# Layer 1 from its second quarter on: scores and sums in four square corners of the TensorE array, even destination blocks before odd ones

## The chip, the core and the metric

The kernel runs on one core of a Trainium2 chip. TensorE (PE) multiplies matrices into the eight banks of PSUM; VectorE (DVE) and ScalarE (ACT) do element work; GpSimd (POOL) and SyncE (SP) issue DMAs here. The metric is the device time of one execution in microseconds (us). The three runs of the kernel before gave 795.45, 795.53 and 796.22, so the median is 795.53.

## The reference, cut to what matters

Four graph layers work on 4096 nodes with 64 features each; every layer normalises its input and adds its result. Layer 0 sums neighbours with decaying weights, layer 1 is an attention, layer 2 is two gated steps, layer 3 is a midpoint in hyperbolic space. The change is in layer 1:

```python
h = lorentz_linear(x, W, b, scale)
q = lorentz_linear(h, Wq, bq, scale_q)
k = lorentz_linear(h, Wk, bk, scale_k)
qm = jnp.concatenate([-q[:, :1], q[:, 1:]], axis=-1)
att = 2.0 + 2.0 * (qm @ k.T)
att = jax.nn.sigmoid(att / att_scale + att_bias)
att = adj * att
support = att @ h
...
return support / denorm
```

`adj` is a dense 4096 x 4096 matrix. The fast path of the kernel needs every entry to be 0 or 1, because it keeps the matrix as 8-bit floats; it checks this on the chip, and falls back on a general path if a check fails.

## The kernel before

**Tiling.** The nodes are 32 blocks of 128 (`NB`), and four quarters of 1024 destinations (`NQ` is 4). A quarter's destinations are dealt out alternately to two halves of 512 columns (`c` = 0 even blocks, `c` = 1 odd blocks; `CW` is 512). `A8[q][i]` holds the adjacency of quarter `q` for the source blocks 2i and 2i+1.

**Layer 1** (`stream1`, from line 1360). For each quarter `q`, pair of source blocks `i` (0 to 15) and half `c`:
- `score` (line 1332) multiplies the keys of two source blocks with the queries of 512 destinations. The contraction is 64 long, so the two blocks use the upper and the lower half of the array's rows (64 rows x 128 columns each) at the same time, into two PSUM banks.
- `weigh` (line 1341) takes two sigmoids on ScalarE out of PSUM and multiplies them by the adjacency on VectorE, into the tile `sig`.
- `add` (line 1364) sums: the source block's 64 features are the columns, so the two blocks use the left and the right half of the array's columns (128 rows x 64 columns each), and add into the two partition halves of the PSUM bank `acc[c]`.

All of these matmuls are in fp32; one such matmul is two records in the trace. The loop takes two pairs `i` at a time: four calls of `score` (both halves, two pairs), then four of `add` for pairs that came earlier, so that the array changes its shape twice a round. `evac` (line 1062) adds the two partition halves of both banks when a quarter is done, and `post1` (line 1417) computes the rest of that quarter, with one transpose before (`ps_n`) and one after (`ps_t`).

**What sets the order.** Everything runs in the order that the program is written in, engine by engine; `Weave` (line 606) writes it. It keeps a planned clock for each engine from fixed costs per operation (`cost`, `book_pe`), and holds side work as generators that yield one operation at a time. `draw` and `fill` insert side work where the plan says that it begins early enough; `finish` issues all that is left of the main side work. `weave.back` is side work of the lowest rank, and is left out while `weave.quiet` is set.

**The checks** (`checks`, line 1113) are that lowest-ranked work. Each of 128 checks loads a 128 x 1024 piece of the adjacency (512 KB, tile `whole`) and has VectorE test that it holds only zeros and ones. The tiles `whole` and `sig` share one pool of six buffers (`b4p`). When layer 3 begins its last part, `layer3` (line 1736) issues every check that is left at once, before its sums go on; after them a small matmul (`flag_ps`) and a copy give the flag that the end of the program reads.

**The end.** Layer 3 computes eight units of 512 destinations. `take3` moves a unit's sums out of PSUM, on ScalarE and then VectorE (`n<-n,acc`; a tile `n65`). `head3` and `post3` (line 1848) then run a long chain of small operations, three units together, then three, then one (unit 6), then the last (`last3`). The Newton steps of a reciprocal root (`guess`, `nt`, `nu`, `ny`) and a polynomial for artanh (`po`, `at`) are in it, and each is one small VectorE instruction after the other.

In the trace, L984 is every matmul (`mm`), L988 every transpose (`turn4`), and L785 every operation that the planner records, so groups are told apart by their tiles.

Of the kernel before, what the change touches and what calls it, by code (L numbers as in the profile page):

```python
# [12 lines left out]
AF = mybir.ActivationFunctionType  # L13
ALU = mybir.AluOpType
# [4 lines left out]
P = 128  # L19
D = 64  # L20
NH = 2
CW = 512
# [13 lines left out]
def general_kernel(ctx: ExitStack, tc: tile.TileContext, t: dict, out: bass.AP):  # L36
# [48 lines left out]

    X = []
    x_nm = t["x"]
    for h in range(NH):
        xh = keep.tile([P, HB, D], F32, name=f"X{h}")
        nc.sync.dma_start(xh, x_nm[:, h * HB:(h + 1) * HB, :])  # L90
        X.append(xh)

# [42 lines left out]
    def nm_tile(name="nm", **kw):  # L135
        return nm.tile([P, HB, D], F32, tag=kw.pop("tag", "nm"), name=name, **kw)

    def stat(name="st"):
        return small.tile([P, HB], F32, tag="st", name=name)
# [5 lines left out]
    def sumsq(v, w=D):  # L145
        sq = nm_tile("sq")
        nc.vector.tensor_tensor(sq[:, :, :w], v, v, ALU.mult)
        s = stat("ss")
        nc.vector.tensor_reduce(s, sq[:, :, :w], AX.X, ALU.add)
        return s  # L150
# [11 lines left out]
    def relu_ln(xh, dst):  # L162

        m = stat("mean")
        nc.vector.tensor_reduce(m, xh, AX.X, ALU.add)
        nc.vector.tensor_scalar(m, m, 1.0 / D, None, op0=ALU.mult)
        xc = nm_tile("xc")
        nc.vector.tensor_tensor(xc, xh, rows(m), ALU.subtract)
        v = sumsq(xc)
        nc.vector.tensor_scalar(v, v, 1.0 / D, LN_EPS, op0=ALU.mult, op1=ALU.add)  # L170
        nc.scalar.activation(v, v, AF.Sqrt)
        nc.vector.scalar_tensor_tensor(dst, xc, 0.0, rows(recip(v)), op0=ALU.max, op1=ALU.mult)
# [20 lines left out]
    def fm_tile(name="fm", **kw):  # L193
        return feat.tile([D + 1, HN], F32, tag=kw.pop("tag", "fm"), name=name, **kw)
# [89 lines left out]
    def pre0(h):  # L284
        hn = nm_tile("h0")
        relu_ln(X[h], hn)
        fm = fm_tile("h0T")
# [282 lines left out]
NQ = 4  # L570
QB = 8
# [30 lines left out]
def names(*aps):  # L602
    return [a.tensor.name for a in aps if isinstance(a, bass.AP)]


class Weave:
# [53 lines left out]
    def free(self, ps):  # L660
        k = ps.tensor.name
        self.banks[self.kind.pop(k)].append(self.used[k][0])
# [7 lines left out]
    def add(self, gen, back=False):  # L670
        piece = [gen, None]
        (self.back if back else self.work).append(piece)
        self.step(piece, None)
# [123 lines left out]
def fast_kernel(ctx: ExitStack, tc: tile.TileContext, t: dict, out: bass.AP, flag: bass.AP):  # L797
# [13 lines left out]
    NB = N // P  # L811
# [10 lines left out]
    weave = Weave()  # L822
    free = weave.free

    def one(name):
        return weave.take(1, lambda: psp.tile([P, CW], F32, tag="one", name=name, bufs=8))

    def several(names_):
        return [one(n) for n in names_]

    def b2(name, shape=(P, QB, D), dtype=F32):
        return b2p.tile(list(shape), dtype, tag="b2", name=name)
# [6 lines left out]
    DV, AC, GP, SY = (Engine(weave, x.e, x.real, True) for x in (V, S_, G_, Y_))  # L839
# [132 lines left out]
    def book_pe(o, lhsT, rhs, passes):  # L972
        k, m, n = lhsT.shape[0], math.prod(lhsT.shape[1:]), math.prod(rhs.shape[1:])
        tiled = (k < P) + 2 * (m < P)
        dur = max(0.42e-3 * n * passes * (0.5 if tiled else 1.0) * (0.5 if k < P and m < P else 1.0), 0.09)
        if passes > 1 and not tiled:
            dur += 0.05 if passes == 2 else 0.075
        weave.book("P", dur + ((0.18 if passes == 4 else 0.115) if tiled != weave.tiled else 0.0), names(lhsT, rhs), names(o))
        weave.tiled = tiled

    def mm(o, lhsT, rhs, start=True, stop=True):
        weave.wait(names(lhsT, rhs), names(o))
        book_pe(o, lhsT, rhs, 4 if lhsT.dtype == F32 else 1)
        nc.tensor.matmul(o, lhsT, rhs, start=start, stop=stop, skip_group_check=True)  # L984
# [31 lines left out]
    def flat(v):  # L1016
        return v.rearrange("p b d -> p (b d)")
# [19 lines left out]
    DONE = set()  # L1037
# [24 lines left out]
    def evac(acc):  # L1062

        lo, hi = slice(0, D), slice(D, P)
        a, mt = b2("agg", (P, CW)), b2("mt", (P, CW))
        sides = ((lo, hi), (hi, lo))
        for ps, (own, other) in zip(acc, sides):
            yield AC.activation(mt[own, :], ps[other, :], AF.Copy)
        for ps, (own, other) in zip(acc, sides):
            yield DV.tensor_tensor(a[own, :], ps[own, :], mt[own, :], ALU.add)  # L1070
            free(ps)
        return a
# [182 lines left out]
    S1, kT = {}, {}  # L1255
# [67 lines left out]
    qd = {}  # L1323

    def load1(q):
        if q < NQ:
            qd[q] = [b2("qd", (P, CW)) for _ in range(2)]
            for c in range(2):
                for half in (slice(0, D), slice(D, P)):
                    Y_.dma_start(qd[q][c][half, :], q_spill[q][c * D:(c + 1) * D, :])  # L1330

    def score(q, i, c):
# [5 lines left out]
            mm(ps[j], kb[half, :], qd[q][c][half, :])  # L1338
        return ps

    def weigh(q, i, c, ps):

        g = b4p.tile([P, 2, CW], F32, tag="b4", name="sig")
        for j in range(2):
            S_.activation(g[:, j, :], ps[j], AF.Sigmoid, bias=att_add, scale=att_mul)
            free(ps[j])
        v = g.rearrange("p k (j n) -> p k j n", n=P)
        a = A8[q][i].rearrange("p k (j c n) -> p k c j n", c=2, n=P)[:, :, c]
        V.tensor_tensor(v, v, a, ALU.mult)
        return g  # L1350
# [9 lines left out]
    def stream1():  # L1360

        acc, behind = [], []

        def add(c, q, i, gs):
            if i == 0:
                acc.append(one(f"acc{c}"))
            for j in range(2):
                b = 2 * i + j
                mm(acc[c][j * D:(j + 1) * D, :], S1[b // QB][:, b % QB, :], gs[c][:, j, :],
                   start=i == 0, stop=i == NB // 2 - 1)  # L1370

        def add_behind(more=()):
            q, i, gs = behind.pop(0)
            for c in (0, 1):
                add(c, q, i, gs)
                if more:
                    more.pop(0)()
                weave.draw(weave.quiet)
            if i == NB // 2 - 1:
                weave.finish()  # L1380
                weave.add(post1(q, acc[:]))
                acc.clear()

        def turn(q, i, later=None):
            if q == 0 and i % (QB // 2) == 0:
                weave.until((1, i // (QB // 2)), DONE)
            weave.quiet = (1, NQ - 1) not in DONE
            weave.late = 2.0 if weave.quiet else 0.8
            gs = ahead[:] if (q, i) == (0, 0) else []
            for c in range(len(gs), 2):  # L1390
                ps = score(q, i, c)
                if later is None:
                    gs.append(weigh(q, i, c, ps))
                else:
                    later.append(lambda q=q, i=i, c=c, ps=ps: gs.append(weigh(q, i, c, ps)))
                weave.draw(weave.quiet or c == 1)
            behind.append((q, i, gs))
            if i == 8:
                load1(q + 1)

        for q in range(NQ):
            for i in range(0, NB // 2, 2):

                later = []
                turn(q, i)
                turn(q, i + 1, later)
                while len(behind) > 2:
                    add_behind(later)
                for go in later:
                    go()  # L1410
                if len(behind) > 1:
                    add_behind()
        add_behind()

    X = {}

    def post1(q, acc):
        a = yield from evac(acc)
        X[q] = b2(f"X{q}")
        yield SY.dma_start(flat(X[q]), x_spill[q])  # L1420
        sup = b2("sup")
        ps = yield from to_nm(a)
        sq = b2("sq")
        yield AC.activation(sq, ps, AF.Square)
        yield AC.activation(sup, ps, AF.Copy)
        free(ps)
        s = stat("space", QB)
        yield DV.tensor_reduce(s, sq[:, :, 1:], AX.X, ALU.add)
        yield DV.tensor_tensor(s, s, sq[:, :, 0], ALU.subtract)
        a = stat("abs", QB)  # L1430
        yield DV.tensor_scalar(a, s, -1.0, 1e-8, op0=ALU.mult, op1=ALU.max)
        yield DV.tensor_tensor(s, s, a, ALU.max)
        r = yield from rsqrt(s)
        yield DV.tensor_tensor(sup, sup, rows(r), ALU.mult)
        yield DV.tensor_tensor(X[q], X[q], sup, ALU.add)

        g = b2("g0")
        yield from relu_ln(X[q], g)
        yield from split3(g, 1.0, *parts(2, q), psum=False)
        DONE.add((2, q))  # L1440
        gT = b2("gT", (P, CW))
        yield from transpose4(g, gT)
        yield from spill2(q, 0, gT)
# [537 lines left out]
```

## Time and profile before

| what | value |
|---|---|
| median of the runs | 795.53 us |
| the profiled execution's own time | 796.44 us |
| its span, first to last instruction | 794.7 us |
| mean granted TensorE clock | 0.993 |
| first score of the second quarter | 305.05 us |
| last matmul record of layer 1's sums, end | 487.49 us |
| sums of layer 3 end, last stretch of TensorE | 779.7 us |
| checks on VectorE | 128, back to back 1.145 us apart |
| load of one check's piece, issue to landing | 6.7 us median |

The durations in the profile are of this one execution. "Busy" is the union of an engine's instructions; matmuls are pipelined, so that the distance between two starts, and not the duration of one, says what a matmul costs in a stream. A row of the timeline merges equal instructions that follow each other: start, length from the first start to the last end, engine, line, operation, what it writes and reads, shape, and count; in brackets, the idle time before it and what ended that. In a table of windows, an engine's number is its busy time, and in parentheses its count of instructions; the last three columns are clock, DMA share and GB/s.

### The profile page before, as it was taken

The numbers are of one execution on the slowest core, as the hardware profiler recorded it, in microseconds if no ns is written. First come the engines' busy times: TensorE is split into PE (matmuls) and PEld (weight loads), VectorE is DVE, ScalarE is ACT, GpSimd is POOL, SyncE is SP. The second block draws the span as 40 slices with busy tenths as digits, with TensorE's granted clock in tenths as the row PEclk, the third lists the DMA queues.
The fourth block names the chain that finished last, engine by engine and source line by source line (L and its number), as shares of the span: only waits on it lengthen the run. The fifth ranks groups of instructions, "written<-read, shape, count | busy, mean of one in ns | idle before, by whom it ended". The sixth has DMA issues, their size and how long they took to land.

```text
span 794.7 us, 12336 instructions
## 1 busy us (share of the span) xinstructions
PE 764.4 (96%) x4494; PEld 370.7 (47%) x4494; DVE 636.3 (80%) x1436; ACT 428.3 (54%) x759; POOL 62.1 (8%) x129
## 2 busy tenths in 40 slices
PE   6899999999999999999999999999999999999992
PEld 2344444444543433333333333444444444699992
DVE  5886867778779888898998997877779678786886
ACT  5565556555567677788787784122220235444333
POOL 4333232232000000000000000000000000000000
PEclk9999999999999999999999999999999999999997
DMA  9999999999710022113103007695788800000000
GB/s 192 162 188 178 222 164 194 220 163 209 203 45 31 10 69 77 41 31 104 53 27 106 27 27 254 202 340 174 254 307 305 287 14 14 2 2 1 15 28 18
DMA packets 44100, 98.54 MB, mean 124 GB/s; under 512 B 5120, under 2 KB 20608, under 8 KB 44032
## 3 DMA queue, kind: packets, MB, share of 16 engines
q1 hardware_dynamic: 25888, 78.98, 29.4%
q0 software_dynamic: 15984, 14.56, 19.6%
q10 hardware_dynamic: 2160, 4.14, 1.4%
q8 instruction: 37, 0.61, 0.3%
q14 instruction: 31, 0.25, 0.1%
HBM read 136.06 MB, written 5.24 MB: 178 GB/s over the span
## 4 chain that ended last, share of the span: by engine, by line
PE 84%; DVE 8%; ACT 3%; DMA 2%; issue 1%; SPq 0%; ACTq 0%; DVEq 0%
PE acc L984 52%; PE score L984 13%; PE cnt L984 12%; PE rz L984 2%; PE ps_l L984 1%; ACT sig L785 1%; PE ps_t L988 1%; DVE ss L785 1%; DVE sig L785 1%; PE ih L984 1%; DMA x<-in_x 1%; DVE nt L785 1%; ACT w L785 1%; PE ps_kq L984 1%; DVE w L785 1%
## 5 line engine op out<-in xcount | busy, mean ns | idle before, releaser
L785 ACT ACTIVATE sig<-score,fatt_add,fatt_mul 128x512 f32<-128x512 f32 x256 | 177.2, 784 | 47.8 <-PE score L984 40.8
L785 DVE TENSOR_TENSOR sig<-sig,A 128x1024 f32<-128x1024 f32 x128 | 155.0, 1224 | 23.5 <-ACT sig L785 17.7
L785 ACT ACTIVATE w<-cnt 128x512 int16<-128x512 f32 x198 | 111.4, 595 | 90.7 <-PE cnt L984 87.8
L785 DVE SCALAR_TENSOR_TENSOR whole<-whole 128x1024 f32<-128x1024 f32 x128 | 153.2, 1220 | 6.3 <-DMA whole<-in_adjT 5.9
L984 PE MATMUL score<-qd,kT 64*128 64x512 f32 x512 | 124.3, 609 | 0.0
L984 PE MATMUL acc<-sig,S 128*64 128x512 f32 x512 | 118.9, 600 | 1.4 <-DVE sig L785 1.2
L984 PEld LDWEIGHTS <-hm 128*128 128x128 bf16 x768 | 73.5, 98 | 92.1 <-issue 9.3
L984 PE MATMUL acc<-A,hm 128*128 128x512 fp8e4 x512 | 115.4, 379 | 0.0
L984 PE MATMUL cnt<-A,ftri 128*128 128x512 fp8e4 x256 | 97.8, 385 | 7.4 <-ACT A L785 5.8
L984 PE MATMUL cnt<-A,fupd 128*128 128x512 fp8e4 x248 | 95.2, 384 | 4.9 <-DVE w L785 1.9
L984 PE MATMUL acc<-S,A 128*128 128x196 bf16 x1024 | 88.4, 246 | 1.3 <-DVE S L785 1.3
L984 PEld LDWEIGHTS <-A 128*128 128x128 fp8e4 x1024 | 87.0, 97 | 2.2 <-DVE S L785 1.5
L984 PEld LDWEIGHTS score<-qd,kT 64*128 64x128 f32 x512 | 50.8, 186 | 68.2 <-issue 55.2
L984 PE MATMUL acc<-w,hm 128*128 128x512 bf16 x256 | 75.5, 379 | 0.3 <-DVE hm L785 0.3
L785 DVE TENSOR_SCALAR w<-cnt 128x512 int16<-128x512 f32 x58 | 40.1, 691 | 39.8 <-PE cnt L984 38.5
L868 POOL DMA_DIRECT2D A<-in_adjT x111 | 60.0, 543 | 129.3 <-DMA A<-in_adjT 128.1
L984 PEld LDWEIGHTS acc<-sig,S 128*64 128x64 f32 x512 | 33.1, 136 | 78.9 <-issue 58.2
L984 PEld LDWEIGHTS <-lo 128*64 128x64 bf16 x768 | 39.6, 109 | 49.6 <-issue 18.8
L984 PE MATMUL acc<-A,lo 128*64 128x512 fp8e4 x512 | 57.9, 380 | 0.0
L785 ACT ACTIVATE mt<-acc 64x512 f32<-64x512 f32 x32 | 18.9, 592 | 64.7 <-PE acc L984 64.1
L984 PEld LDWEIGHTS <-ftri 128*128 128x128 bf16 x256 | 24.8, 98 | 45.3 <-issue 21.2
L984 PEld LDWEIGHTS <-fupd 128*128 128x128 bf16 x248 | 24.4, 98 | 38.4 <-issue 14.0
(187 smaller groups left out, 611.5 us busy)
## 6 DMA issues: line engine op xcount, KB each, us to landing
whole<-in_adjT SPq DMA_DIRECT2D x128, 512.0 KB, 6.7
A<-in_adjT POOLq DMA_DIRECT2D x111, 128.0 KB, 13.7
qd<-qs SPq DMA_DIRECT2D x16, 128.0 KB, 4.9
mx<-gs SPq DMA_DIRECT2D x16, 128.0 KB, 8.0
xT<-gs SPq DMA_DIRECT2D x8, 256.0 KB, 7.4
x<-in_x SPq DMA_DIRECT2D x6, 256.0 KB, 6.7
xs<-x SPq DMA_DIRECT2D x4, 256.0 KB, 5.9
qs<-qT ACTq DMA_DIRECT2D x4, 256.0 KB, 4.5
```

The lines of the kernel that those rows point to most:

```text
L785: return fn(*args, **kw)
L868: nc.gpsimd.dma_start(A8[q][b // 2][:, b % 2, :], a)
L984: nc.tensor.matmul(o, lhsT, rhs, start=start, stop=stop, skip_group_check=True)
L988: nc.tensor.transpose(o, src, ident)
```

## The change

The first quarter stays as it is. From the second quarter on, a new function `rest` runs the stream:

- `score4` cuts a pair's score matmuls into four of 64 rows x 64 columns: row half `r` is the source block as before, column half `h` is half of its 128 nodes. The two banks come out as before.
- `sum4` cuts the sums into four of 64 x 64: row half `r` is half of a source block's nodes, column half `k % 2` is the block of the pair. Bank `r` receives the sums over its half of the nodes; the result of one half of destinations is now spread over both banks and both partition halves.
- All even destination blocks of a quarter (`c` = 0, all 16 pairs) run first, then all odd ones.
- One score group and one sum group alternate; the sums run three steps behind the scores.
- `evac4` runs twice a quarter and adds the four partial sums together: a ScalarE copy of a bank (128 x 512), a VectorE sum, a ScalarE copy across partition halves (64 x 512), a VectorE sum. `evac` ran once, with two ScalarE copies and two VectorE sums of 64 x 512.
- `weave.quiet` and `weave.late` are set once, before `rest`; `load1` for the next quarter is called at the start of the odd blocks.

```diff
+    corners = [(slice(r * D, (r + 1) * D), slice(h * D, (h + 1) * D)) for r in range(2) for h in range(2)]
+
+    def score4(q, i, c):
+
+        kb = kT[i // 4][:, (i % 4) * P:(i % 4 + 1) * P]
+        ps = several(("score", "score"))
+        for j, (r, h) in enumerate(corners):
+            mm(ps[j // 2][h, :], kb[r, h], qd[q][c][r, :])
+        return ps
+
+    def sum4(acc, i, g):
+
+        for k, (r, h) in enumerate(corners):
+            b = 2 * i + k % 2
+            mm(acc[k // 2][h, :], S1[b // QB][r, b % QB, :], g[r, k % 2, :],
+               start=i == 0, stop=i == NB // 2 - 1)
...
+        def rest():
...
+            def close(q, c, ps):
+                if c == 0:
+                    halves[q] = b2("agg", (P, CW))
+                    weave.add(evac4(halves[q], ps, c))
+                else:
+                    weave.finish()
+                    weave.add(post1(q, ps))
...
+            for q in range(1, NQ):
+                for c in (0, 1):
+                    for i in range(NB // 2):
+                        g = weigh(q, i, c, score4(q, i, c))
+                        weave.draw(False)
+                        sums.append(lambda q=q, c=c, i=i, g=g: sums_of(q, c, i, g))
+                        if len(sums) > 3:
+                            pop()
+                        if (c, i) == (1, 0):
+                            load1(q + 1)
+            while sums:
+                pop()
+
+        for q in range(1):
...
-        add_behind()
...
+        weave.until((1, NQ - 1), DONE)
+        weave.quiet, weave.late = False, 0.8
+        rest()
...
+    def evac4(a, acc, c):
+
+        own, other = [slice(0, D), slice(D, P)][::1 - 2 * c]
+        t = b2("mt", (P, CW))
+        yield AC.activation(t, acc[0], AF.Copy)
+        free(acc[0])
+        yield DV.tensor_tensor(t, acc[1], t, ALU.add)
+        free(acc[1])
+        yield AC.activation(a[own, :], t[other, :], AF.Copy)
+        yield DV.tensor_tensor(a[own, :], t[own, :], a[own, :], ALU.add)
+
     def post1(q, acc):
-        a = yield from evac(acc)
+        if q in halves:
+            a = halves[q]
+            yield from evac4(a, acc, 1)
+        else:
+            a = yield from evac(acc)
```

More of the change, by code (lines that the diff above doesn't have):

```diff
@@ L1378, in add_behind @@
                 weave.draw(weave.quiet)
[L1379 to L1382, printed above, removed]
         def turn(q, i, later=None):
@@ L1398, in turn, with last, sums_of, pop @@
             if i == 8:
-                load1(q + 1)
-        for q in range(NQ):
+                load1(1)
+        def rest():
+            q0, i0, gs = behind.pop(0)
+            def last():
+                add(1, q0, i0, gs)
+                weave.finish()
+                weave.add(post1(q0, acc[:]))
+                acc.clear()
+            sums = [lambda: add(0, q0, i0, gs), last]
+            def close(q, c, ps):
[3 more added lines that the diff above has]
+                else:
+                    weave.finish()
+                    weave.add(post1(q, ps))
+            def sums_of(q, c, i, g):
+                if i == 0:
+                    acc[:] = several(("acc0", "acc1"))
+                sum4(acc, i, g)
+                if i == NB // 2 - 1:
+                    close(q, c, acc[:])
+                    acc.clear()
+            def pop():
+                sums.pop(0)()
+                weave.draw()
+            for q in range(1, NQ):
[11 more added lines that the diff above has]
+        for q in range(1):
             for i in range(0, NB // 2, 2):
@@ L1412, in stream1 @@
                     add_behind()
-        add_behind()
-    X = {}
-    def post1(q, acc):
-        a = yield from evac(acc)
+        weave.until((1, NQ - 1), DONE)
+        weave.quiet, weave.late = False, 0.8
+        rest()
+    X, halves = {}, {}
+    def evac4(a, acc, c):
[7 more added lines that the diff above has]
+        yield DV.tensor_tensor(a[own, :], t[own, :], a[own, :], ALU.add)
+    def post1(q, acc):
+        if q in halves:
[3 more added lines that the diff above has]
+            a = yield from evac(acc)
         X[q] = b2(f"X{q}")
```

## The prediction

> **What bounds the kernel now.** I read the page first (busy time, chain), then layer 1 on TensorE in order of time, then the VectorE queue at the very end. The page and its chain of waits:
>
> ```profile
> PE 764.4 (96%) x4494; PEld 370.7 (47%) x4494; DVE 636.3 (80%) x1436; ACT 428.3 (54%) x759; POOL 62.1 (8%) x129
> ...
> PE 84%; DVE 8%; ACT 3%; DMA 2%; issue 1%; SPq 0%; ACTq 0%; DVEq 0%
> ...
> L984 PE MATMUL score<-qd,kT 64*128 64x512 f32 x512 | 124.3, 609 | 0.0
> L984 PE MATMUL acc<-sig,S 128*64 128x512 f32 x512 | 118.9, 600 | 1.4 <-DVE sig L785 1.2
> ...
> 305.05:487.42 182.37, 182.27 (x803) 66.71 (x801) 163.67 (x222) 144.99 (x217) 0.00 (x0) 1.00 0.19 59
> ```
>
> TensorE sets the pace, and in the stretch that changes (305.05, the first score of the second quarter, to 487.42, the first sum of layer 2) it has no gap at all. VectorE is busy 90% and ScalarE 80% of that stretch. Now the same stretch matmul by matmul, and a group of layer 2's gates that already uses four square corners:
>
> ```profile
> 304.52 0.60 PE L984 MATMUL acc<-sig,S 128*64 128x512 f32 x2
> ...
> 305.05 0.70 PE L984 MATMUL score<-qd,kT 64*128 64x512 f32 x2
> ...
> 305.58 1.02 PE L984 MATMUL score<-qd,kT 64*128 64x512 f32 x4
> ...
> 307.73 1.02 PE L984 MATMUL score<-qd,kT 64*128 64x512 f32 x3
> ...
> 308.30 0.59 PE L984 MATMUL score<-qd,kT 64*128 64x512 f32 x1
> ...
> 308.82 0.65 PE L984 MATMUL acc<-sig,S 128*64 128x512 f32 x2
> ...
> 309.30 1.03 PE L984 MATMUL acc<-sig,S 128*64 128x512 f32 x4
> ...
> 531.30 0.66 PE L984 MATMUL ih<-mx,g 64*64 64x512 f32 x4
> ...
> 531.78 0.61 PE L984 MATMUL ih<-mx,g 64*64 64x512 f32 x4
> ...
> 532.32 0.41 PE L984 MATMUL acc<-A,lo 128*64 128x512 fp8e4 x2
> ```
>
> A matmul record here is half of an fp32 matmul and lasts 0.59. Four records (two starts of two) end 1.02 after the first, so starts are 1.02 - 0.59 = 0.43 apart: one score pair or one sum pair costs two starts, 0.86. Around a change of shape the starts are 0.53 and 0.53 (sums to scores: 0.20 over) and 0.52 and 0.48 (scores to sums: 0.14 over). At 307.73 three start and the fourth only at 308.30: one half of the last pair came 0.14 late. The gate group: four corners start together, the next four 0.48 later, like the first sum pair, and the next work 0.54 after that.
>
> Last, the end of the VectorE queue, where the checks of the adjacency (`whole`) stand:
>
> ```profile
> 730.57 1.22 DVE L785 SCALAR_TENSOR_TENSOR whole<-whole 128x1024 f32<-128x1024 f32 x1
> ...
> 732.04 0.16 DVE L785 TENSOR_TENSOR odds<-odds,odd 128x1 f32<-128x1 f32 x1
> 733.09 0.14 DVE L785 CAST flag<-flag_ps 1x1 int32<-1x1 f32 x1 [0.89 <-PE flag_ps L984]
> ...
> 742.07 0.61 DVE L785 TENSOR_TENSOR n<-n,acc 128x130 f32<-128x130 f32 x2 [1.98 <-ACT alpha L785]
> ...
> 781.33 0.48 DVE L785 TENSOR_TENSOR n<-n,acc 128x65 f32<-128x65 f32 x2
> ...
> 789.00 0.42 DVE L785 TENSOR_TENSOR X<-X,n 128x256 f32<-128x256 f32 x1
> ```
>
> One check is left at 730.57, and VectorE idles only 3.9 us between 732.2 and 781.33 (0.89, 0.15, 1.98, 0.24 and 0.61, each waiting for another engine's result).
>
> **What the Trainium skill says.** "TensorEngine Tiling (Array Packing)", Key Properties: changing the tiling mode drains TensorE, while tiles of one mode work in parallel. The trace agrees: 0.09 to 0.10 late at each change, the rest of the overhead being the first weight load. "TensorE: Matmul & The Clock Gate", LDWEIGHTS: a load's time goes with its columns, not its rows; here 187 ns for 128 and 137 ns for 64 fp32 columns, so the corner's first load shows as the sums' does (0.05). Tiling page, PSUM Bottleneck: evacuation can become the bound once TensorE is faster; hence the budget below. The TensorE page's opening table: VectorE's queue is strict FIFO; so whatever stands behind a block of checks waits for it.
>
> **The change, part by part.** *Array work.* The number of full-array groups stays: 96 score and 96 sum groups of three quarters, plus two sums left of the first, 194 x 0.859 (0.43 rounded up from 0.4295 per start) = 166.6 of the 182.4. The remaining 15.7: 24 rounds x (0.20 + 0.14 + 0.14) = 11.5, and six transposes of 0.7 = 4.2. Scores and sums in the same 64x64 shape lose the changes; alternating one score with one sum asks for two banks at a time instead of eight, so the late half goes too. What comes instead: five changes while the first quarter's last sums mix with the first corner scores, 5 x 0.14 = 0.7; six transposes, now always between corner groups, 6 x 0.73 = 4.4; about 0.5 at the six handovers of sum banks, when four banks instead of six serve the scores; 0.5 at the end, where the last sum waits for its mask. 15.7 - 6.1 = **9.6 saved, I take 9.5**. The corner start distance in a long stream isn't in the trace (only two starts in a row). Upper bound of the gain: 15.7 - 5.1 = 10.6. Lower: each ns on the start distance costs 388 starts x 1 ns = 0.39; layer 3 issues a load and a matmul every 85 ns (548 in 46.76 in the timeline), 43 per instruction, and corners need 8 per 430 ns, 54 each, so I add nothing; 10 ns more would cost 3.9.
>
> *ScalarE and VectorE beside it.* A step is now 1.72. ScalarE has two sigmoids of 0.67 (four in 2.79 with the last 0.78), VectorE one mask product of 1.145. The new evacuation runs twice a quarter: a 128x512 and a 64x512 on each of both engines (0.6 and 0.69 each), four operations per engine a quarter where two stood, so +1.2 on ScalarE and +1.4 on VectorE. Adding the built order's rows between masks: VectorE 151 and ScalarE 145 of 165. Score to sum is six groups, 5.15; sigmoids and mask take 3.0; the largest VectorE queue by these sums is 2.3 (once), against 2.1 of slack. Hidden, except for the 0.5 above; if the cover goes, up to 1 per quarter.
>
> *Checks.* This is the part that the diff doesn't show. The built order puts 14 checks between the masks of the last three quarters before, and 3 after: VectorE no longer has holes that the planner sees. Layers 2 and 3 take one more than before (67 for 66). So where one check is forced at 730.57, eleven stand in a row: ten more, each 1.145 (eight in a row start at that distance from 505.32 on). VectorE comes 11.5 later to the last layer's sums. TensorE isn't stopped: its flag matmul now stands 180 matmuls behind, 180 x 0.085 = 15.3, and the block ends after 13.3; nor do the PSUM banks of that layer run out (the fourth unit's are wanted 192 x 0.085 = 16.3 after the restart at 730.32, and freed at 13.3 + four sums of 0.3 = 14.6).
>
> *The end.* From the checks (732.2) to the last sum (781.33, 51.0 after the restart) VectorE had 49.1 us, 3.9 of them idle. Now it has 51.0 - 13.3 = 37.7. The planner answers by order: behind the last `n<-n,acc` stood 38 instructions, now 74. Those added, with their durations from the trace of before: closing the last group of three 2.9 (766.7 to 770.9 less the two sums between), preparing unit 6 1.0, its Newton steps 2.1, its artanh 1.9: 7.9, of which about 1 goes by interleaving: **6.9**. Cross-check: 49.1 - 3.9 - 7.9 = 37.3 fits in 37.7, so VectorE reaches the last sum in time, and the tail alone is longer. Bounds 5.5 (better interleaved) and 9.5 (VectorE 2.6 late).
>
> *Sum.* -9.5 + 6.9 = -2.6 on the profiled execution: span 794.7 to 792.1, time 796.44 to 793.8. That execution is 0.9 above the median of the runs shown, 795.53; for that I say **792.9**.
>
> **Rivals.** *Nothing given back* (0.10): VectorE swallows the checks in its idle time and the full 9.5 stays, 786.0. For it, TensorE ends the chain; against it, only 3.9 idle and 36 more instructions behind the last sum. *Checks paced by their transfers* (0.13), the slower one: only six buffers exist, so five of the eleven loads start when a check ends. Late in layer 2 such checks stood 1.3 to 2.0 apart (615.65 to 623.74). If the seven that aren't among the four loaded early take 1.9 each, the block is 5.3 longer, passes the flag matmul and delays the last sum by as much: 798.2. It decides from 2.6 us, that is 1.5 per such check. Against it: eight stood back to back earlier. *Corners a little slower than pairs* (0.12): 20 ns per start costs 7.8, 800.7; slower than before from 6.7 ns on. Against it: the gate group's 0.48 equals the sums' first start. *Layer 1 meets ScalarE or VectorE* (0.15): saved 5 instead of 9.5, 797.4 at the worst end, 796 in the middle.
>
> **How the numbers follow.** The likeliest case has 0.50 and its own range 790.5 to 795.5. For 8 in 10 I reach toward both sides: 788.5 to 799. Under 0.2% (1.6 us) this measurement can't tell from no change. Faster: 0.43 of the likeliest, all of the first rival, 0.02 of the last: 0.55. Same: 0.07 + 0.13: 0.20. Slower: 0.25.
>
> **What would show it.** Right: starts of 0.43 throughout the corner stretch with no 0.52 but at transposes, the stretch 173 instead of 182; first sum of layer 2 near 478; eleven checks in a row near 721; last TensorE sum near 770 and some 15 us of VectorE from there, where 8 were. Wrong: starts of 0.45 or more, idle before `sig` or `score` that names ACT or DVE, a `flag_ps` wait, or checks that name DMA.

## The result, and the profile after

| | before | after |
|---|---|---|
| median of 11 runs each | 795.67 us | 793.80 us (793.09 to 794.64) |
| ratio of the times | | 0.9976, 95% interval 0.9967 to 0.9985 |
| profiled execution's own time, span | 796.44, 794.7 | 794.03, 792.2 |
| first sum of layer 2 | 487.42 | 476.83 |
| last sum of layer 3 ends on TensorE | 779.74 | 769.89 |
| from there to the end | 14.9 | 22.3 |

The changed kernel is 0.24% faster. Layer 1 gives 10.6 us, and 7.4 of them come back behind the last matmul. The page of the changed kernel shows this as a shift in the chain of waits, from TensorE to VectorE (84% and 8% before); the groups of scores and sums have one shape from the second quarter on, and a group of four corner matmuls is eight records:

```profile
PE 751.9 (95%) x5241; PEld 364.6 (46%) x5262; DVE 636.0 (80%) x1442; ACT 435.8 (55%) x765; POOL 62.0 (8%) x129
...
PE 79%; DVE 12%; ACT 3%; DMA 2%; issue 2%; SPq 0%; ACTq 0%; DVEq 0%
...
L984 PE MATMUL acc<-sig,S 64*64 64x512 f32 (+1 forms) x896 | 130.8, 592 | 1.4 <-DVE sig L785 1.2
L984 PE MATMUL score<-qd,kT 64*64 64x512 f32 (+1 forms) x896 | 131.6, 594 | 0.0
```

VectorE has as much work as before (636.0 and 636.3) and TensorE 12.5 less, so neither busy time tells why only 2 us are gained. Read in order of time it is plain. The timeline of TensorE, in the middle of the corner stretch and from layer 3's last part to the end:

```profile
330.04 1.04 PE L984 MATMUL acc<-sig,S 64*64 64x512 f32 x8
330.90 1.04 PE L984 MATMUL score<-qd,kT 64*64 64x512 f32 x8
331.76 1.04 PE L984 MATMUL acc<-sig,S 64*64 64x512 f32 x8
332.62 1.04 PE L984 MATMUL score<-qd,kT 64*64 64x512 f32 x8
...
719.73 15.55 PE L984 MATMUL acc<-S,A 128*128 128x196 bf16 x180 [1.31 <-DVE S L785]
735.94 0.19 PE L984 MATMUL flag_ps<-fones,odds 128*1 128x1 f32 x2 [0.67 <-DVE n L785]
736.06 33.83 PE L984 MATMUL acc<-S,A 128*128 128x196 bf16 x396
```

A group of eight records starts every 0.86 (330.04, 330.90, 331.76), whether it is scores or sums: the pairs took as long, and there is no loss at the change from one to the other. TensorE's last part begins behind a wait for `S`, the tile with the sources of layer 3's sums; this start is called the restart below, and the time behind TensorE's last sum the tail. The same part in the kernel before:

```profile
730.32 2.61 PE L984 MATMUL acc<-S,A 128*128 128x196 bf16 x28 [1.31 <-DVE S L785]
732.86 0.19 PE L984 MATMUL flag_ps<-fones,odds 128*1 128x1 f32 x2
732.98 46.76 PE L984 MATMUL acc<-S,A 128*128 128x196 bf16 x548
```

The restart at 719.73 is 10.59 earlier than there (730.32), with the same wait of 1.31. Then the flag matmul stops TensorE for 0.67 where it hadn't. The table of windows has the corner stretch, from the first corner score to the first sum of layer 2 (columns as before: the span, then PE, PEld, DVE, ACT and POOL):

```profile
304.59:476.83 172.24, 172.02 (x1570) 60.79 (x1569) 153.23 (x208) 152.25 (x222) 0.00 (x0) 1.00 0.11 34
```

It lasts 172.2 where it was 182.4. VectorE and ScalarE are now busy 89% and 88% of it, and a planner that fills holes finds few: 3 checks between the masks of these three quarters, where 13 were. The end of the checks on VectorE, and its last operations:

```profile
728.01 1.22 DVE L785 SCALAR_TENSOR_TENSOR whole<-whole 128x1024 f32<-128x1024 f32 x1
...
730.31 1.23 DVE L785 SCALAR_TENSOR_TENSOR whole<-whole 128x1024 f32<-128x1024 f32 x1 [1.07 <-DMA whole<-in_adjT]
...
731.59 1.23 DVE L785 SCALAR_TENSOR_TENSOR whole<-whole 128x1024 f32<-128x1024 f32 x1
...
733.63 1.22 DVE L785 SCALAR_TENSOR_TENSOR whole<-whole 128x1024 f32<-128x1024 f32 x1 [0.80 <-DMA whole<-in_adjT]
...
735.10 0.16 DVE L785 TENSOR_TENSOR odds<-odds,odd 128x1 f32<-128x1 f32 x1
735.18 1.14 DVE L785 TENSOR_TENSOR n<-n,acc 128x130 f32<-128x130 f32 x4
...
771.70 0.48 DVE L785 TENSOR_TENSOR n<-n,acc 128x65 f32<-128x65 f32 x2
...
786.43 0.42 DVE L785 TENSOR_TENSOR X<-X,n 128x256 f32<-128x256 f32 x1
```

Eleven checks stand in a row from 719.99, eight of them 1.145 apart. The last three come late by 1.15, 0.13 and 0.90 (730.31, 731.59 and 733.63 against the end of the check ahead, 1.145 after its start), twice because their data has not landed. VectorE reaches the last sum in time (771.70, TensorE ended at 769.89), but from that sum's start to the end of its work are 15.15 us, where 8.09 were (781.33 to 789.42).

The account in the spans: layer 2 starts 10.59 earlier, TensorE's last part takes 0.74 longer (50.16 against 49.42), and what follows is 7.39 longer (22.31 against 14.92): -2.46, and the spans differ by 2.45.

### The profile page after: what moved, and what is told of

Its sections match the earlier page's. It is cut to its first block, busy times and chain, and to the rows that moved or that the text cites. A ratio compares the mean times of both kernels' runs of the same rounds, so it can differ in the third digit from the quotient of the medians.

```text
span 792.2 us, 13872 instructions
## 1 busy us (share of the span) xinstructions
PE 751.9 (95%) x5241; PEld 364.6 (46%) x5262; DVE 636.0 (80%) x1442; ACT 435.8 (55%) x765; POOL 62.0 (8%) x129
## 4 chain that ended last, share of the span: by engine, by line
PE 79%; DVE 12%; ACT 3%; DMA 2%; issue 2%; SPq 0%; ACTq 0%; DVEq 0%
PE acc L984 47%; PE score L984 13%; PE cnt L984 12%; DVE n L785 2%; PE rz L984 2%; DVE ss L785 2%; PE ps_l L984 1%; DMA whole<-in_adjT 1%; PE ps_t L988 1%; DVE whole L785 1%; DVE sig L785 1%; DVE nt L785 1%; PE ih L984 1%; ACT sig L785 1%; DMA x<-in_x 1%
## 5 line engine op out<-in xcount | busy, mean ns | idle before, releaser
L785 ACT ACTIVATE sig<-score,fatt_add,fatt_mul 128x512 f32<-128x512 f32 x256 | 182.8, 776 | 31.4 <-PE score L984 25.6
L785 DVE TENSOR_TENSOR sig<-sig,A 128x1024 f32<-128x1024 f32 x128 | 155.2, 1222 | 24.2 <-ACT sig L785 22.3
L984 PE MATMUL acc<-sig,S 64*64 64x512 f32 (+1 forms) x896 | 130.8, 592 | 1.4 <-DVE sig L785 1.2
L984 PE MATMUL score<-qd,kT 64*64 64x512 f32 (+1 forms) x896 | 131.6, 594 | 0.0
L984 PEld LDWEIGHTS score<-qd,kT 64*64 64x64 f32 (+1 forms) x896 | 41.1, 140 | 67.6 <-issue 57.5
L984 PE MATMUL acc<-w,hm 128*128 128x512 bf16 x235 | 70.4, 379 | 1.2 <-DVE hm L785 0.4
L984 PEld LDWEIGHTS acc<-sig,S 64*64 64x64 f32 (+1 forms) x896 | 36.8, 133 | 74.9 <-issue 47.7
L785 ACT ACTIVATE mt<-acc 64x512 f32<-64x512 f32 (+1 forms) x32 | 19.0, 592 | 64.1 <-PE acc L984 63.6
L984 PEld LDWEIGHTS <-fupd 128*128 128x128 bf16 x248 | 24.3, 98 | 37.9 <-issue 13.3
```

The source lines that it names most:

```text
L785: return fn(*args, **kw)
```

## The experiments

Times are medians of four runs or more, beside runs of the kernel before on the same chip (795.66 to 796.05 by chip).

**The end without its checks.** The changed kernel, without the last 11 of 128 (so the flag says nothing of those pieces):

```diff
-        todo = [(b, q) for n, (q, b) in enumerate(tiles) if not direct(n)]
+        todo = [(b, q) for n, (q, b) in enumerate(tiles) if not direct(n)][:-11]
```

> The changed kernel with the last 11 of the 128 checks of the adjacency left out, so that no check stands in layer 3's last part; all else is as it was. Theory (layer 1 saved 10 us, and the checks that VectorE no longer fits in give 7 of it back at the end): the VectorE tail behind TensorE's last sum falls from 15.2 to about 8, the wait of 0.67 before flag_ps goes, and the time is about 786.5, 7.3 less than the changed kernel. Rival (the tail is longer because of how the planner now orders the last units, and not because of the checks): 793 to 794, with the tail still near 15.

Measured: 790.24 (ratio to before 0.9936, 0.9920 to 0.9953). The time behind TensorE's last sum fell from 22.31 to 14.94, as expected, but 3.6 us of gain are half of 7.3. TensorE's timeline of this run around the restart:

```profile
711.72 6.96 PE L984 MATMUL acc<-S,A 128*128 128x196 bf16 x80
722.38 50.58 PE L984 MATMUL acc<-S,A 128*128 128x196 bf16 x576 [3.70 <-DVE S L785]
```

And its table of windows from there (the third column from the end is the granted clock):

```profile
722.38:725.40 3.02, 3.02 (x19) 2.81 (x20) 0.35 (x1) 0.18 (x2) 0.00 (x0) 0.50 0.00 0
725.40:740.00 14.60, 14.60 (x174) 14.59 (x173) 10.59 (x42) 4.49 (x17) 0.00 (x0) 1.00 0.00 1
```

The planner, with no checks left, put the flag matmul and the last projections elsewhere in TensorE's order: 80 sums instead of 108 stand behind the last projection, so the wait for `S` grew from 1.31 to 3.70 and the restart came 2.65 later. After that wait the clock is at half for 3 us: 18 starts are 163 ns apart instead of 85, some 1.4 us in all. The first edit was thus not clean: it also moved the work ahead.

**The control.** The same edit in the kernel before.

> The kernel before with the same 11 of 128 checks left out: there they stand in VectorE's idle time. Theory: the same time as the kernel before, 795.0 to 796.0, since only one check stood in the last part and the tail is 8 already. Rival (leaving out checks helps by itself, through less DMA traffic or less VectorE work anywhere): 2 us or more less, and then e1's gain is not the end block's alone.

Measured: 799.95 (1.0053, 1.0037 to 1.0070), slower, which neither theory had. Leaving work out helped nothing here, and moved the order in the same way, as TensorE's timeline of this run shows:

```profile
720.62 7.99 PE L984 MATMUL acc<-S,A 128*128 128x196 bf16 x92
731.29 50.67 PE L984 MATMUL acc<-S,A 128*128 128x196 bf16 x576 [2.69 <-DVE S L785]
```

Its table of windows:

```profile
731.29:734.40 3.11, 3.11 (x20) 2.85 (x21) 0.35 (x1) 0.27 (x2) 0.00 (x0) 0.50 0.00 0
```

The restart is 0.97 later than before (16 sums fewer behind the last projection, 16 x 0.085 = 1.4), and the half clock costs another 1.5 (less 0.2, since the flag matmul has left the last part). A further 0.8 lies behind the last VectorE operation, and its cause stays open. The span is 3.1 longer in all, and the median 4.3: the profiled execution of the kernel before lay 0.8 above the median of the runs beside this one (796.44 against 795.66).

**Only the block taken away.** So that the plan ahead stays as it is, the checks are dropped at the very point where they are forced; one runs, as in the kernel before, but the small sums that pass its result to the flag fall away too:

```diff
+    drop = []
...
             yield DV.scalar_tensor_tensor(a, a, 0.0, a, op0=ALU.not_equal, op1=ALU.not_equal,
                                           accum_out=odd[:, j:j + 1])
+            if drop:
+                break
...
         weave.quiet = False
+        drop.append(True)
         while weave.back and weave.back[0][1].e == "D":
```

> The changed kernel in which, of the eleven checks that layer 3's last part would force, only the first runs and ten are dropped at that very point, so that the plan of everything ahead of it stays as it is (118 of 128 checks). Theory (the ten checks in a row cost the tail 7.1 and the flag's wait 0.7, and nothing else differs): restart of TensorE still after a wait of 1.31, no wait before flag_ps, tail behind TensorE's last sum 15 us to the end instead of 22.3, time 785.5 to 786.7. Rival (the tail comes from elsewhere, and the first run's gain of 3.6 was all there is to have): 790 or more.

Measured: 785.29 (0.9866, 0.9850 to 0.9883). TensorE's timeline has the same 108 sums ahead of the restart, the flag matmul ahead of it too, and no stop after it:

```profile
708.73 9.34 PE L984 MATMUL acc<-S,A 128*128 128x196 bf16 x108
718.00 0.19 PE L984 MATMUL flag_ps<-fones,odds 128*1 128x1 f32 x2
719.39 49.20 PE L984 MATMUL acc<-S,A 128*128 128x196 bf16 x576 [1.20 <-DVE S L785]
```

Behind the last `n<-n,acc` stand 38 VectorE instructions, as before the change, against 74. The tail is 14.95 us. The changed kernel takes 8.5 us more (8.7 in the spans: 7.4 of tail, 1.0 in TensorE's last part, and 0.3 that this execution was ahead at the first sum of layer 2 already, 476.50 against 476.83, where the edit does nothing yet). Against the kernel before, the run is 10.6 us faster, which is what layer 1 gave. This settles that the checks gave the gain back.

**Checks pushed to the end in the kernel before.** The array work of layer 1 is untouched; only its checks are held back. In layer 1, and in the list of pieces:

```diff
-        return self.work[:self.width] + ([] if self.quiet else self.back)
+        return self.work[:self.width] + ([] if self.quiet or self.hold else self.back)
...
+            weave.hold = q > 0
...
+        weave.hold = False
```

> The kernel before, whose layer 1 is unchanged, but with no check issued in layer 1's last three quarters: 17 checks then stand in a row in layer 3's last part. Theory (checks that find no room in layer 1 are paid at the end): the block is 17 x 1.145 = 19.5 long and some 4 more by late transfers, VectorE reaches the last sum with some 17 us more of work behind it: 808 to 815. Rival (VectorE's idle time takes them in): under 800.

Measured: 812.83 (1.0216, 1.0199 to 1.0233), as the theory said. The 17 checks take from 729.66 to 752.26 and TensorE stops for the sums behind them; the last row is its table of windows from there:

```profile
729.40 16.56 PE L985 MATMUL acc<-S,A 128*128 128x196 bf16 x192 [1.32 <-DVE S L786]
753.35 13.19 PE L985 MATMUL acc<-S,A 128*128 128x196 bf16 x128 [7.39 <-DVE n L786]
...
753.35:757.80 4.45, 4.45 (x28) 4.08 (x29) 4.18 (x17) 1.11 (x7) 0.00 (x0) 0.50 0.01 4
```

It stops after exactly 192 sums, three units of 64, 16.6 us after the restart: the point that the prediction worked out for the fourth unit's banks. So here the order of the halves and the corners play no part, and the loss is the same in kind.

**The order without the corners.** `score4` and `sum4` keep their order and get back the old shapes, and the second evacuation bank goes:

```diff
-        for j, (r, h) in enumerate(corners):
-            mm(ps[j // 2][h, :], kb[r, h], qd[q][c][r, :])
+        for j in range(2):
+            half = slice(j * D, (j + 1) * D)
+            mm(ps[j], kb[half, :], qd[q][c][half, :])
...
-        for k, (r, h) in enumerate(corners):
-            b = 2 * i + k % 2
-            mm(acc[k // 2][h, :], S1[b // QB][r, b % QB, :], g[r, k % 2, :],
+        for j in range(2):
+            b = 2 * i + j
+            mm(acc[0][j * D:(j + 1) * D, :], S1[b // QB][:, b % QB, :], g[:, j, :],
...
```

> The changed order alone: one score group and one sum group alternately, even destinations first, three steps behind, but in the old shapes (scores 64 x 128 in pairs, sums 128 x 64 in pairs into one bank). Theory (the gain of the change is the shape that scores and sums now share): the array changes shape twice in each of 96 steps, 0.20 + 0.14 = 0.34 each, 32.6 in layer 1 where the kernel before paid 24 x 0.34 = 8.2 in the same part; VectorE then has room for more checks in layer 1, and the tail is short again: 814 to 828. Rival (the gain comes from the order and from needing two banks at a time instead of eight): 796 or less.

Measured: 820.55 (1.0317, 1.0300 to 1.0334). The same piece of layer 1 on TensorE:

```profile
330.21 1.13 PE L984 MATMUL score<-qd,kT 64*128 64x512 f32 x4
331.27 1.08 PE L984 MATMUL acc<-sig,S 128*64 128x512 f32 x4
332.28 1.13 PE L984 MATMUL score<-qd,kT 64*128 64x512 f32 x4
```

A step of one score and one sum lasts 2.07 (330.21 to 332.28), in corners 1.72: 0.35 for the two changes of shape, where 0.34 had been read from the profile of before. Layer 2 starts at 507.68, 30.9 later than in corners. VectorE then has room for every check ahead of the last part, and the tail is 15.0 again. TensorE's restart in this run comes after a wait of 2.69, as in the control, and yet at the full clock (1.00 from 752.22 to 755.20 in its table of windows):

```profile
752.22 49.20 PE L984 MATMUL acc<-S,A 128*128 128x196 bf16 x576 [2.69 <-DVE S L785]
```

The fine alternation pays only because scores and sums share a shape.

**Corners without even-first.** Both halves of a pair follow each other, so that four banks hold sums (the rest of the edit keeps the sums of the two halves apart and moves the next quarter's load to the middle of this one):

```diff
-                for c in (0, 1):
-                    for i in range(NB // 2):
+                for i in range(NB // 2):
+                    for c in (0, 1):
...
```

> The changed kernel with even and odd destinations of a pair of source blocks one after the other instead of all even ones first, so that sums hold four PSUM banks instead of two and scores have four instead of six. Theory (the shared shape makes the gain; the order of the halves only decides how many banks are free, and two at a time are enough): layer 1 as long as in the changed kernel to within 1 us, 14 checks in the last block instead of 11, so a tail and block 3 to 5 longer: 796 to 800. Rival (even-first is what makes it fast): scores wait for sigmoids to free banks, layer 1 is 5 us longer or more, and 801 or more.

Measured: 807.39 (1.0145, 1.0128 to 1.0162); both numbers of the theory were too small. In the first of the three quarters the groups start 0.86 apart as ever; at the two places where these quarters meet, they fall into two pieces. TensorE's timeline at the first such place and at layer 3's last part, and its table of windows behind the second wait:

```profile
372.20 0.98 PE L984 MATMUL score<-qd,kT 64*64 64x512 f32 x4
372.63 0.60 PE L984 MATMUL acc<-sig,S 64*64 64x512 f32 x2
373.02 0.60 PE L984 MATMUL score<-qd,kT 64*64 64x512 f32 x2
373.06 0.98 PE L984 MATMUL acc<-sig,S 64*64 64x512 f32 x4
...
722.55 16.56 PE L984 MATMUL acc<-S,A 128*128 128x196 bf16 x192 [1.32 <-DVE S L785]
742.06 6.56 PE L984 MATMUL acc<-S,A 128*128 128x196 bf16 x56 [2.95 <-DVE n L785]
...
742.20:745.40 3.20, 3.20 (x22) 2.96 (x21) 2.96 (x13) 1.11 (x7) 0.00 (x0) 0.50 0.00 0
```

Layer 2 starts 2.66 later than in the changed kernel, not under 1 (that late banks split the groups fits, but no row names them). And 14 checks instead of 11 cost 9.9 more, not 3 to 5: the last of them ends 18.4 after the restart, past the 16.6 at which the banks run out, so TensorE stops for 2.95 after 192 sums and comes back at half the clock for 3.2 us, 20 starts of 163 ns, which costs another 1.6; its last part is 54.2 instead of 50.2 and the rest 28.2 instead of 22.3.

**Room for the checks, one edit.** In the changed kernel the program keeps checks out of layer 3's first part:

```diff
             if step and q == NQ - 1:
-                weave.quiet = True
+                pass
```

> The changed kernel in which the checks may also be issued in layer 3's first part, where the program kept them out; the planner puts seven of the eleven there, and four are left for the last part. Theory (only the checks of the last part cost, and VectorE waits for TensorE in the first part): the block shrinks from 15.5 to about 5, the tail from 15.2 to about 10, no wait before flag_ps, and the time is 788 to 790. Rival (a check in the first part stands ahead of the work that TensorE waits for at the restart of the last part, where it already waits 1.31): that wait grows by what the tail gives back, 792 to 796.

Measured: 788.41 (0.9911, 0.9894 to 0.9927), as the theory said. Four checks are left for the block, the tail is 16.6, and the wait at the restart is 1.89 instead of 1.31: the rival's mechanism is there, at 0.6 us.

```profile
720.54 6.36 PE L984 MATMUL acc<-S,A 128*128 128x196 bf16 x72 [1.89 <-DVE S L785]
```

**Room for all checks.** On top of it, after layer 1:

```diff
         rest()
+        weave.late = 1.6
```

> As v1, and the planner may also let side work on VectorE end 1.6 us instead of 0.8 past its time from layer 2 on, so that all 128 checks are issued before layer 3's last part. Theory: no block, no flag wait, tail near 15 us to the end, and the restart of the last part waits for nothing, since 144 sums of the last part instead of 108 are queued behind the last projection: 784 to 786. Rival (the checks now stand ahead of work that TensorE waits for in layer 2 and the first part of layer 3): waits of TensorE of 3 us or more there, 788 or more.

Measured: **783.91** (0.9852, 0.9835 to 0.9868), every check is done, and it beats both kernels: 1.5% below the one before, 9.9 us below the changed one. TensorE's timeline from the last projection on has no wait at all:

```profile
705.38 2.55 PE L984 MATMUL acc<-S,A 128*128 128x196 bf16 x28
707.86 0.19 PE L984 MATMUL flag_ps<-fones,odds 128*1 128x1 f32 x2
707.98 58.99 PE L984 MATMUL acc<-S,A 128*128 128x196 bf16 x692
```

The wait of 1.31 is gone too, since 144 sums (28 + 692 - 576) now cover the last chain on VectorE.

**The same two edits in the kernel before.** `weave.late = 1.6` follows its layer 1 too.

> The kernel before with the same two planner edits as v2. Theory (what v2 gains is what the change had given back, so there is little of it to gain here): only the one forced check and the wait of 1.31 at the restart can go, 793 to 795, and v2 is 9 to 10 below it, which is then the worth of the corners with nothing given back. Rival (the planner edit helps by itself whatever layer 1 does): 788 or less.

Measured: 794.40 (0.9980, 0.9973 to 0.9988): 1.5 us. So the edits are worth little where nothing had been given back, and the corners and their order, with nothing given back, are worth 794.40 - 783.91 = 10.5 us.

## Why the prediction was right, point by point

The median was put at 792.9 and is 793.80; the profiled execution at 793.8 with a span of 792.1, and was 794.03 with 792.2. The 0.9 at the median comes from one term: the prediction took off 0.9 because the profiled execution of before stood that far above its median, while the one of after stands only 0.23 above its own.

- *Layer 1 saved 9.5*: the stretch gave 182.37 - 172.24 = 10.1, and the start of layer 2, which also has the 0.46 by which the second quarter began earlier, 10.6. Two terms were sized too high. The 0.5 for handing over sum banks is nothing: outside of changes of shape, transposes and the end no two starts are more than 0.44 apart. The wait for the last mask costs 0.40, not 0.5. The six transposes cost 0.74 each (0.73 put), the changes of shape 0.15 each (0.14 put). That corners start like pairs, on which the rival of 20 ns stood, holds to the third digit: six groups in 5.15, 0.858 each.
- *ScalarE and VectorE beside it* hid as put: no score waits, and in the whole of layer 1 the sums wait for masks 1.2 us, 1.0 of it in the first quarter, as before.
- *Eleven checks in a row* came as the built order showed. (By the trace 13 and 3 checks stand between the masks, and 67 behind them up to the last part in both kernels; the prediction's 14 and 66 put one check on the other side of that border, and the ten come out the same.) *The block ends 13.3 after the restart* is the step that failed: it ends 15.5 after, with `odds`. The rival that checks are paced by their transfers was half right, with three late checks (2.2 us) where it priced seven (5.3). The Trainium skill, "TensorE: Matmul & The Clock Gate", opening table, has VectorE's queue as strict FIFO; what that costs is in the timeline, since `odds` and the sums behind the block move with its last check.
- *TensorE isn't stopped* failed with it: the flag matmul stands 180 sums = 15.5 behind the restart, and TensorE stopped 0.67 there (the last part is 0.74 longer). The row names `n`, not `odds`, and the times agree: `odds` ended at 735.26, the second of the sums behind the block at 735.79, and the flag matmul began 0.15 after that one. The stops of 2.95 and 7.39 in the other two runs end 0.15 after the same second sum. So what the flag matmul waited for is, by the trace, not its input but the PSUM bank that this sum frees; it takes one of the eight itself, and the prediction counted banks only for the fourth unit. No run tests this alone. *The banks of that layer don't run out* held for that unit, and its limit of 16.3 showed itself as 16.6 in the two runs whose block passed it.
- *The tail, +6.9*: VectorE's own, 15.15 against 8.09, is +7.06, with 74 instructions against 38 behind the last sum. The 3.9 of idle time in the cross-check leaves out two gaps of VectorE in the kernel before, 0.28 at 767.13 and 0.49 at 780.24; with them the check has more room, and VectorE did reach the last sum in time. Dropping ten checks brings the time behind TensorE's last sum from 22.3 back to 15.0, so the cause is shown, not only the size.

Of the rivals, *nothing given back* (786.0) is close to what the run with ten checks dropped shows (785.3), but VectorE doesn't swallow them where they stand, and *corners slower than pairs* and *layer 1 meets ScalarE or VectorE* find nothing in the trace. Two of the prediction's signs of being wrong did come, a `flag_ps` wait of 0.67 and two checks that name DMA, 1.9 in all.

Layer 2's earlier start (10.6 where 9.5 was put) and the losses (0.74 in the last part where nothing was put, 7.4 behind TensorE's end where 6.9 was) nearly cancel: 1.1 against 1.2. So the sum came closer than its terms by luck.

## What to carry to other kernels

Scores and sums that alternate on TensorE are worth one common tile shape: each change of shape here cost 0.14 to 0.20 us, and the shared shape, with the order that it allows, saved 10.5 us once nothing was given back. But a planner with cheap work of low rank turns a faster stretch into a debt: count where that work goes in the built order, and give it a place in idle time ahead of the last stretch before judging the edit. And an experiment that leaves work out has to leave the order ahead of it as it is, or it measures the planner.

## What the runs showed of the hardware that was not expected

After some waits TensorE came back at half the granted clock: 0.50 for 3.0 us after a wait of 3.70, for 3.1 after 2.69, for 3.2 after 2.95, and for 4.4 after 7.39 (starts of 163 ns instead of 85). After waits of 1.2 to 1.9, and after another of 2.69 in the run of the order alone, it did not (1.00 from the restart on). The Trainium skill, "TensorE: Matmul & The Clock Gate", Part 1, describes such a gate, with windows of about 3.4 us that run freely and half the clock after one idle window. Windows that run freely fit that the same 2.69 once cost 1.5 us and once nothing; but 2.69 and 2.95 are shorter than the page's window and were enough, and there the measurement stands.

The second finding is that a late block isn't paid in proportion: 4, 11, 14 and 17 checks in the last part went with 16.6, 22.3, 28.2 and 22.2 us behind TensorE's last sum, and the longest tail is not the one with the most checks. Up to 11 TensorE stopped for at most 0.67, then for 2.95 and 7.39; the tail goes with the number of VectorE instructions behind the last `n<-n,acc`: 38 where one check or none was left (14.6 to 15.8), 50 with four, 74 with eleven and with seventeen, and 105 with fourteen. Why the planner leaves fewer there with seventeen checks than with fourteen, these runs do not take apart.
